# Cross-attention on one core: the context width as 128 + 64 rows instead of 96 + 96, with the 64-row products alternating between the two halves of TensorE's rows

## The chip, the cores and the metric

One NeuronCore of a Trainium2 chip runs the whole program. The metric is device time in microseconds (us) of one execution, as the median of several runs. TensorE (PE in the profile) does the matrix products, from SBUF into PSUM; VectorE (DVE) and ScalarE (ACT) empty PSUM and do the elementwise work; GpSimd (POOL) does one multiplication per tile; SyncE (SP) issues most transfers.

## What is computed

Everything is float32: 16 batches, 256 queries of width 256, 77 context rows of width 192, 8 heads of width 256.

```
Q = (img_embed @ Wq)   K = (sent_embed @ Wk)   V = (sent_embed @ Wv)     # 8 heads each
score = jnp.einsum('bhqd,bhkd->bhqk', Q, K) / math.sqrt(D)
score = jnp.where(mask, score, -jnp.inf)
attn = jax.nn.softmax(score, axis=-1)
ctx = jnp.einsum('bhqk,bhkd->bqhd', attn, V).reshape(B, -1, H * D)
out = ctx @ Wo + img_embed
mu = jnp.mean(out, axis=-1, keepdims=True)
var = jnp.var(out, axis=-1, keepdims=True)
return (out - mu) * jax.lax.rsqrt(var + EPS) * gamma + beta
```

## The kernel before

Neither Q, K, V nor the context of a head is formed. Per head h the kernel takes, once, `G_h = Wq_h Wk_h^T / sqrt(D)` and `U_h = Wv_h Wo_h`. Then, for a batch b, `A_bh = G_h c_b^T` (tile `a`) and `VW_bh = c_b U_h` (tile `vw`); the scores are `x_b A_bh` and the output is the sum over heads of `softmax(score) VW_bh`.

The products `a` and `vw` sum over the context width, 192. The kernel before takes it in two chunks of `LP` = 96 rows, so each of these products is two matmuls into one PSUM bank. A float32 matmul is two instructions on TensorE (each a weight load and a pass that streams the moving operand); a transpose is one. "Pass" below means one such instruction. So a product of `a` or `vw` is four passes.

The program has two parts.

- **Once** (lines 97 to 189): per head, transposes of Wq and Wk (`p_wqT`, `p_wkT`), their copies to SBUF, then `pg` (8 passes) and one copy of it into `gT`; six tiles of transposes of the context (`pc`), each with two copies into `cT`; per head, a transpose of Wv (`p_wvT`), `pu` (8 passes) and one copy into `u`.
- **The batches** (lines 192 to 336), in 32 steps t of 128 queries, two for each batch, eight for each group of four batches. At the first step of a group, `prepare_group` transposes x (`px`) and makes the 16 products `pa` of 308 columns, each copied by ACT or DVE in turn into `a`. Each step takes the scores (`ps`, 8 passes, two banks), then on DVE the bias is added (this reads `ps`), the maximum is taken and subtracted, ACT takes the exponential `e`, DVE the sum and reciprocal, POOL the product `p`. At each even step `prepare_batch` makes four products `pv` of 512 columns, each copied by ACT into `vw`. Two steps later `attend` transposes `p` (`pp`, two tiles of four), ACT copies them to `pT`, and `po` (16 passes) sums the heads; DVE adds x. `normalise_group` and the stores follow once a group.

Each engine runs its instructions in program order, which the scheduler of the language fixes when the kernel is built, by the order of the code, priorities and free buffers. PSUM has eight banks: `ps_sc` two buffers of two banks (scores), `ps_tr` two of one bank (all transposes), `ps_mm` two of one bank (`pg`, `pu`, `pa`, `pv`, `po`). A matmul into a buffer waits until the copy out of it is done.

Of the kernel before, what the change touches and what calls it, by code (L numbers as in the profile page):

```python
# [8 lines left out]
F32 = mybir.dt.float32  # L9
I32 = mybir.dt.int32  # L10
AF = mybir.ActivationFunctionType
ALU = mybir.AluOpType
AX = mybir.AxisListType
PSUM = bass.MemoryType.PSUM

P = 128
H = 8          # heads
D = 256        # head width
EPS = 1e-05
GB = 4         # batches in a group  # L20
MASKED = 3.0e38  # taken from a masked score: any score of less than 1e31 is absorbed by it


# Per head h the products are taken in this order:
#   G_h = Wq_h Wk_h^T / sqrt(D)        U_h = Wv_h Wo_h        (once)
#   A_bh = G_h c_b^T                   VW_bh = c_b U_h        (once a batch)
#   score_bh = x_b A_bh                out_b = sum_h softmax(score_bh) VW_bh
# so neither Q, K, V nor the context of a head is ever formed.
@with_exitstack
def kernel(  # L30
    ctx: ExitStack,
# [12 lines left out]
    nc = tc.nc  # L44
    B, S, DI = x.shape
    S2, DL = c.shape[1], c.shape[2]
    LP = DL // 2               # the context width goes in two chunks of LP rows
    CR = 112                   # rows of the flat context in one transpose
    NCR = B * S2 // CR
    NG = B // GB  # L50
    QT = S // P                # query tiles of a batch
    NT = B * QT
    GT = GB * QT               # query tiles of a group
    HK = H // 2 * S2           # score columns in one PSUM bank
    assert NCR * CR == B * S2 and NG * GB == B and DI == 2 * P and D == 2 * P

    const = ctx.enter_context(tc.tile_pool(name="const", bufs=1))
    xp = ctx.enter_context(tc.tile_pool(name="xp", bufs=2))
    ps_sc = ctx.enter_context(tc.tile_pool(name="ps_sc", bufs=2, space=PSUM))
    ps_tr = ctx.enter_context(tc.tile_pool(name="ps_tr", bufs=2, space=PSUM))  # L60
    ps_mm = ctx.enter_context(tc.tile_pool(name="ps_mm", bufs=2, space=PSUM))

    ident = const.tile([P, P], F32, tag="ident", name="ident")
    make_identity(nc, ident)
    eps = const.tile([P, 1], F32, tag="eps", name="eps")
    nc.vector.memset(eps, EPS)

    gT = const.tile([LP, 2, H, DI], F32, tag="gT", name="gT")
    u = const.tile([LP, 2, H, DI], F32, tag="u", name="u")
    cT = const.tile([LP, 2, B * S2], F32, tag="cT", name="cT")  # L70
    bias = const.tile([P, B, S2], F32, tag="bias", name="bias")
    live = const.tile([P, B], F32, tag="live", name="live")
    gam = const.tile([P, DI], F32, tag="gam", name="gam")
# [15 lines left out]
    def evacuate(dst, src):  # L89
        evacs[0] += 1  # L90
        if evacs[0] % 2:
            nc.scalar.copy(dst, src)  # L92
        else:
            nc.vector.tensor_copy(dst, src)  # L94

# [1 line left out]
    with tc.tile_pool(name="wload", bufs=1) as wp, tc.tile_pool(name="wt", bufs=2) as wt:  # L97
        wq_sb = wp.tile([P, 2, H * D], F32, tag="wq", name="wq_sb")
        wk_sb = wp.tile([LP, 2, H * D], F32, tag="wk", name="wk_sb")
        wv_sb = wp.tile([LP, 2, H * D], F32, tag="wv", name="wv_sb")  # L100
        wo_sb = wp.tile([P, 2 * H, DI], F32, tag="wo", name="wo_sb")
        c_sb = wp.tile([CR, NCR, DL], F32, tag="c", name="c_sb")
        m_i = wp.tile([P, B * S2], I32, tag="mi", name="m_i")
        wq_r = wq.rearrange("(t p) f -> p t f", p=P)
        wk_r = wk.rearrange("(t p) f -> p t f", p=LP)
        wv_r = wv.rearrange("(t p) f -> p t f", p=LP)
        half = H * D // 2
        for i in range(2):
            cols = slice(i * half, (i + 1) * half)
# [26 lines left out]
        for h in range(H):  # L136
            wqT = transposed(wq_sb, P, h, "wqT")
            wkT = transposed(wk_sb, LP, h, "wkT")
            pg = ps_mm.tile([P, 2, DI], F32, tag="mm", name=f"pg_{h}")
            for lc in range(2):  # L140
                for dc in range(2):
                    nc.tensor.matmul(  # L142
                        pg[:LP, lc, :],
                        wkT[:, dc, lc * LP : (lc + 1) * LP],
                        wqT[:, dc, :],
                        start=(dc == 0),
                        stop=(dc == 1),
                    )
            nc.scalar.mul(gT[:, :, h, :], pg[:LP], D ** -0.5)

        for r in range(0, NCR, 2):
            n = min(2, NCR - r)
            pc = ps_tr.tile([P, 4, P], F32, tag="tr", name=f"pc_{r}")
            for lc in range(2):
                for j in range(n):
                    nc.tensor.transpose(
                        pc[:LP, 2 * lc + j, :CR],
                        c_sb[:, r + j, lc * LP : (lc + 1) * LP],
                        ident[:CR, :CR],
                    )  # L160
            for lc in range(2):
                evacuate(
                    cT[:, lc, r * CR : (r + n) * CR].rearrange("p (j m) -> p j m", m=CR),
                    pc[:LP, 2 * lc : 2 * lc + n, :CR],
                )

        for h in range(H):
            wvT = transposed(wv_sb, LP, h, "wvT")
            pu = ps_mm.tile([P, 2, DI], F32, tag="mm", name=f"pu_{h}")
            for lc in range(2):  # L170
                for dc in range(2):
                    nc.tensor.matmul(  # L172
                        pu[:LP, lc, :],
                        wvT[:, dc, lc * LP : (lc + 1) * LP],
                        wo_sb[:, 2 * h + dc, :],
                        start=(dc == 0),
                        stop=(dc == 1),
                    )
            evacuate(u[:, :, h, :], pu[:LP])

        # bias: 0 where the mask is nonzero, -MASKED where it is zero, which exp takes to 0.
        # live: 1 for a batch with an unmasked column, else 0 / 0, the NaN of the reference.
        bias_f = bias.rearrange("p b k -> p (b k)")
        nc.vector.tensor_scalar(bias_f, m_i, 0.0, None, ALU.not_equal)
        some = wp.tile([P, B], F32, tag="some", name="some")
# [2 lines left out]
        nc.vector.tensor_tensor(live, live, some, ALU.mult)  # L188
        nc.vector.tensor_scalar(bias_f, bias_f, 1.0, MASKED, ALU.subtract, ALU.mult)

# [1 line left out]
    ap = ctx.enter_context(tc.tile_pool(name="ap", bufs=2))  # L192
    sp = ctx.enter_context(tc.tile_pool(name="sp", bufs=3))
    st = ctx.enter_context(tc.tile_pool(name="st", bufs=4))
# [3 lines left out]
    def prepare_group(g):  # L198
        xg = xg_of[g]
        xT = xp.tile([P, 2, GT * P], F32, tag="xT", name=f"xT_{g}")  # L200
        for j in range(0, GT, 2):
            pt = ps_tr.tile([P, 4, P], F32, tag="tr", name=f"px_{g}_{j}")
            for dc in range(2):
                for i in range(2):
                    nc.tensor.transpose(  # L205
                        pt[:, 2 * dc + i, :], xg[:, j + i, dc * P : (dc + 1) * P], ident
                    )
            evacuate(
                xT[:, :, j * P : (j + 2) * P],
                pt.rearrange("p (dc i) m -> p dc (i m)", dc=2),  # L210
            )
        xT_of[g] = xT
        a = ap.tile([P, 2, GB, H, S2], F32, tag="a", name=f"a_{g}")
        for h in range(H):
            for dc in range(2):
                pa = ps_mm.tile([P, GB, S2], F32, tag="mm", name=f"pa_{g}_{h}_{dc}")
                for lc in range(2):
                    nc.tensor.matmul(  # L218
                        pa.rearrange("p b k -> p (b k)"),
                        gT[:, lc, h, dc * P : (dc + 1) * P],  # L220
                        cT[:, lc, g * GB * S2 : (g + 1) * GB * S2],
                        start=(lc == 0),
                        stop=(lc == 1),
                    )
                evacuate(a[:, dc, :, h, :], pa)
        a_of[g] = a
        mv_of[g] = st.tile([P, GT, 2], F32, tag="mv", name=f"mv_{g}", bufs=2)

    def prepare_batch(b):
        vw = ap.tile([S2, H, DI], F32, tag="vw", name=f"vw_{b}", bufs=3)  # L230
        for n in range(H // 2):
            pv = ps_mm.tile([P, 2 * DI], F32, tag="mm", name=f"pv_{b}_{n}")
            for lc in range(2):
                nc.tensor.matmul(  # L234
                    pv[:S2],
                    cT[:, lc, b * S2 : (b + 1) * S2],
                    u[:, lc, 2 * n : 2 * n + 2, :].rearrange("p h d -> p (h d)"),
                    start=(lc == 0),
                    stop=(lc == 1),
                )  # L240
            nc.scalar.copy(vw[:, 2 * n : 2 * n + 2, :].rearrange("p h d -> p (h d)"), pv[:S2])  # L241
        vw_of[b] = vw

    def scores_and_softmax(t):
# [78 lines left out]
    for t in range(NT + AHEAD):  # L323
# [6 lines left out]
        if t >= AHEAD:  # L330
            d = t - AHEAD
# [36 lines left out]
```

## Time and profile before

| | |
|---|---|
| median of 3 runs | 482.4 us (482.24 to 482.61) |
| span of the profiled execution, first to last instruction | 480.1 us |
| median less span | 2.3 us |
| TensorE busy | 439.0 us, 91% of the span |
| VectorE, ScalarE, GpSimd busy | 210.7, 136.8 and 39.6 us |
[...]

The profiled execution has no time of its own in the results beside its span; 2.3 us is what lies around the span if it ran like the median. Busy time of TensorE includes the modelled end of each matmul, so it doesn't tell how much of that time is needed.

### The profile page before, as it was taken

The numbers are of one execution on the slowest core, as the hardware profiler recorded it, in microseconds if no ns is written. First come the engines' busy times: TensorE is split into PE (matmuls) and PEld (weight loads), VectorE is DVE, ScalarE is ACT, GpSimd is POOL, SyncE is SP. The second block draws the span as 40 slices with busy tenths as digits, with TensorE's granted clock in tenths as the row PEclk, the third lists the DMA queues.
The fourth block names the chain that finished last, engine by engine and source line by source line (L and its number), as shares of the span: only waits on it lengthen the run. The fifth ranks groups of instructions, "written<-read, shape, count | busy, mean of one in ns | idle before, by whom it ended". The sixth has DMA issues, their size and how long they took to land.

```text
span 480.1 us, 4689 instructions
## 1 busy us (share of the span) xinstructions
PE 439.0 (91%) x1846; PEld 298.3 (62%) x1846; DVE 210.7 (44%) x424; ACT 136.8 (28%) x242; POOL 39.6 (8%) x38
## 2 busy tenths in 40 slices
PE   1409899999999999999999999999999999999993
PEld 1307677755765875758567766585767756658572
DVE  0031223235736433375373433844735238555364
ACT  1103422223132222251333213523132134331321
POOL 0000000012112000121111101112111011121110
PEclk9859999999999999999999999999999999999997
DMA  8993000000000000022000000130000000200002
GB/s 237 256 341 106 0 1 1 0 2 0 0 1 0 1 0 0 1 87 89 0 0 1 0 0 2 53 123 0 1 1 0 1 0 1 89 0 0 2 1 87
DMA packets 13446, 17.86 MB, mean 37 GB/s; under 512 B 480, under 2 KB 12208, under 8 KB 13232
## 3 DMA queue, kind: packets, MB, share of 16 engines
q1 hardware_dynamic: 9696, 12.95, 8.9%
q10 hardware_dynamic: 3728, 4.62, 3.3%
q8 instruction: 14, 0.23, 0.2%
q14 instruction: 8, 0.07, 0.0%
HBM read 13.37 MB, written 4.19 MB: 37 GB/s over the span
## 4 chain that ended last, share of the span: by engine, by line
PE 87%; DMA 6%; DVE 3%; ACT 2%; issue 0%; DVEq 0%; ACTq 0%
PE po L293 24%; PE pv L234 22%; PE pa L218 14%; PE ps L250 14%; PE pp L289 5%; DMA m_i<-in_mask_BxS_if_dram 5%; PE pg L142 3%; PE pu L172 3%; DMA wk_sb<-in_L_xattn_Wk_dram 2%; PE px L205 2%; DVE wkT L94 1%; ACT pT L290 1%; DVE xg L313 1%; PE p_wkT L126 0%; PE p_wvT L126 0%
## 5 line engine op out<-in xcount | busy, mean ns | idle before, releaser
L293 PE MATMUL po<-vw,pT 77*128 77x256 f32 x512 | 117.2, 382 | 1.7 <-ACT pT L290 1.7
L234 PE MATMUL pv<-u,cT 96*77 96x512 f32 x256 | 113.1, 593 | 0.1
L293 PEld LDWEIGHTS po<-vw,pT 77*128 77x128 f32 x512 | 94.6, 190 | 21.3 <-ACT pT L290 9.7
L234 PEld LDWEIGHTS pv<-u,cT 96*77 96x77 f32 x256 | 37.5, 148 | 67.0 <-issue 57.8
L250 PE MATMUL ps<-a,xT 128*128 128x308 f32 x256 | 75.8, 422 | 0.0
L277 POOL TENSOR_TENSOR p<-e,rden 128x616 f32<-128x616 f32 x32 | 38.9, 1216 | 423.1 <-DVE rden L275 236.5
L218 PE MATMUL pa<-cT,gT 96*128 96x308 f32 x256 | 67.7, 422 | 0.0
L241 ACT COPY vw<-pv 77x512 f32<-77x512 f32 x64 | 37.1, 581 | 97.8 <-PE pv L234 97.5
L297 DVE TENSOR_TENSOR xg<-po,xg 128x256 f32<-128x256 f32 x32 | 13.6, 424 | 108.8 <-PE po L293 108.7
L290 ACT COPY pT<-pp 77x512 f32<-77x512 f32 x64 | 34.1, 583 | 86.5 <-PE pp L289 86.5
L218 PEld LDWEIGHTS pa<-cT,gT 96*128 96x128 f32 x256 | 48.0, 190 | 16.6
L250 PEld LDWEIGHTS ps<-a,xT 128*128 128x128 f32 x256 | 46.5, 190 | 12.4 <-issue 0.5
L289 PEld LDWEIGHTS pp<-ident,p 128*77 128x77 f32 x256 | 30.4, 148 | 11.3 <-issue 5.3
L94 DVE COPY a<-pa 128x308 f32<-128x308 f32 x32 | 15.3, 479 | 48.1 <-PE pa L218 48.1
L272 DVE TENSOR_REDUCE den<-e 128x8 f32<-128x616 f32 x32 | 25.4, 794 | 23.5 <-ACT e L270 23.4
L142 PE MATMUL pg<-wqT,wkT 128*96 128x256 f32 x64 | 18.9, 447 | 18.2 <-DVE wkT L94 18.2
L289 PE MATMUL pp<-ident,p 128*77 128x128 f32 x256 | 33.2, 272 | 0.0
L258 DVE TENSOR_TENSOR s<-ps,bias 128x616 f32<-128x616 f32 x32 | 25.6, 799 | 10.7 <-PE ps L250 10.7
L270 ACT ACTIVATE e<-s 128x616 f32<-128x616 f32 x32 | 22.9, 717 | 23.5 <-DVE s L266 23.4
L92 ACT COPY a<-pa 128x308 f32<-128x308 f32 x32 | 13.4, 418 | 48.3 <-PE pa L218 48.3
L142 PEld LDWEIGHTS pg<-wqT,wkT 128*96 128x96 f32 x64 | 11.6, 192 | 23.5 <-DVE wkT L94 19.8
L266 DVE TENSOR_TENSOR s<-s,top 128x616 f32<-128x616 f32 x32 | 25.6, 800 | 1.0
(45 smaller groups left out, 212.8 us busy)
## 6 DMA issues: line engine op xcount, KB each, us to landing
xg<-in_x_dram SPq DMA_DIRECT2D x4, 1024.0 KB, 12.5
out_dram<-xg SPq DMA_DIRECT2D x16, 256.0 KB, 2.2
wq_sb<-in_L_xattn_Wq_dram SPq DMA_DIRECT2D x2, 1024.0 KB, 12.3
wo_sb<-in_L_xattn_Wo_dram ACTq DMA_DIRECT2D x1, 2048.0 KB, 39.0
wk_sb<-in_L_xattn_Wk_dram ACTq DMA_DIRECT2D x2, 768.0 KB, 11.3
wv_sb<-in_L_xattn_Wv_dram SPq DMA_DIRECT2D x1, 1536.0 KB, 22.1
c_sb<-in_ctx_dram ACTq DMA_DIRECT2D x1, 924.0 KB, 27.3
m_i<-in_mask_BxS_if_dram SPq DMA_DIRECT2D x1, 616.0 KB, 21.7
```

The costliest lines, as they stand in the source:

```text
L142: nc.tensor.matmul(pg[:LP, lc, :], wkT[:, dc, lc * LP : (lc + 1) * LP], wqT[:, dc, :], start=(dc == 0), stop=(dc == 1),)
L218: nc.tensor.matmul(pa.rearrange("p b k -> p (b k)"), gT[:, lc, h, dc * P : (dc + 1) * P], cT[:, lc, g * GB * S2 : (g + 1) * GB * S2], star ...
L234: nc.tensor.matmul(pv[:S2], cT[:, lc, b * S2 : (b + 1) * S2], u[:, lc, 2 * n : 2 * n + 2, :].rearrange("p h d -> p (h d)"), start=(lc == 0 ...
L241: nc.scalar.copy(vw[:, 2 * n : 2 * n + 2, :].rearrange("p h d -> p (h d)"), pv[:S2])
L250: nc.tensor.matmul(ps[:, hh, :HK], xT_of[g][:, dc, j * P : (j + 1) * P], a_of[g][:, dc, bl, hh * 4 : hh * 4 + 4, :].rearrange("p h k -> p ...
L258: nc.vector.tensor_tensor(s.rearrange("p (a h) k -> p a h k", a=2), ps[:, :, :HK].rearrange("p a (h k) -> p a h k", k=S2), bias[:, b, :].u ...
L266: nc.vector.tensor_tensor(s, s, top.unsqueeze(2).to_broadcast([P, H, S2]), ALU.subtract)
L272: nc.vector.tensor_reduce(den, e, AX.X, ALU.add)
L277: nc.gpsimd.tensor_tensor(p, e, rden.unsqueeze(2).to_broadcast([P, H, S2]), ALU.mult)
L289: nc.tensor.transpose(pt[:S2, i, :], p[:, hh * 4 + i, :], ident)
L290: nc.scalar.copy(pT[:, hh * 4 : hh * 4 + 4, :], pt[:S2])
L293: nc.tensor.matmul(po, pT[:, h, :], vw_of[b][:, h, :], start=(h == 0), stop=(h == H - 1))
```

## The change

The context width goes in one chunk of 128 rows (`gA`, `uA`, `cA`) and one of 64 (`gB`, `uB`, `cB`). A product of `a` or `vw` is a matmul over 128 rows and one over 64 rows. The 64-row operands stand in rows 0 to 63 or in rows 64 to 127: `gB` by the head's parity, `uB` by the parity of the pair of heads, and `cB` in both halves. Products are made four at a time, in four banks: first the four 128-row matmuls, then the four 64-row ones, whose halves alternate from one matmul to the next, then the four copies. `ps_mm` gets four buffers, and `ps_sc` one instead of two. In the first part each PSUM tile of `pg`, `pu` and `pc` is emptied by two or three copies instead of one or two. `ps`, `pp`, `po` and the softmax are as before.

```
-    ps_sc = ctx.enter_context(tc.tile_pool(name="ps_sc", bufs=2, space=PSUM))
+    ps_sc = ctx.enter_context(tc.tile_pool(name="ps_sc", bufs=1, space=PSUM))
-    ps_mm = ctx.enter_context(tc.tile_pool(name="ps_mm", bufs=2, space=PSUM))
+    ps_mm = ctx.enter_context(tc.tile_pool(name="ps_mm", bufs=4, space=PSUM))
...
-                        pg[:LP, lc, :],
-                        wkT[:, dc, lc * LP : (lc + 1) * LP],
+                        pg[:, lc, :],
+                        wkT[:, dc, lc * LB : lc * LB + P],
...
-            nc.scalar.mul(gT[:, :, h, :], pg[:LP], D ** -0.5)
+            nc.scalar.mul(gA[:, h, :], pg[:, 0, :], D ** -0.5)
+            half = slice(h % 2 * LB, h % 2 * LB + LB)
+            nc.vector.tensor_scalar(gB[half, h // 2, :], pg[LB:, 1, :], D ** -0.5, None, ALU.mult)
...
+            evacuate(cA[:, rows].rearrange("p (j m) -> p j m", m=CR), pc[:, :n, :CR])
+            for i in range(2):
                 evacuate(
-                    cT[:, lc, r * CR : (r + n) * CR].rearrange("p (j m) -> p j m", m=CR),
-                    pc[:LP, 2 * lc : 2 * lc + n, :CR],
+                    cB[i * LB : (i + 1) * LB, rows].rearrange("p (j m) -> p j m", m=CR),
+                    pc[LB:, 2 : 2 + n, :CR],
                 )
...
-            evacuate(u[:, :, h, :], pu[:LP])
+            evacuate(uA[:, h, :], pu[:, 0, :])
+            n = h // 2
+            evacuate(uB[n % 2 * LB : n % 2 * LB + LB, n // 2, h % 2, :], pu[LB:, 1, :])
...
+        for n in range(H // 2):
+            parts = [(dc, i) for dc in range(2) for i in range(2)]
+            pa = {
+                (dc, i): ps_mm.tile([P, GB, S2], F32, tag="mm", name=f"pa_{g}_{2 * n + i}_{dc}")
+                for dc, i in parts
+            }
+            for dc, i in parts:
+                nc.tensor.matmul(
+                    pa[dc, i].rearrange("p b k -> p (b k)"),
+                    gA[:, 2 * n + i, dc * P : (dc + 1) * P],
+                    cA[:, cols],
+                    start=True,
+                    stop=False,
+                )
+            for dc, i in parts:
+                half = slice(i * LB, (i + 1) * LB)
+                nc.tensor.matmul(
+                    pa[dc, i].rearrange("p b k -> p (b k)"),
+                    gB[half, n, dc * P : (dc + 1) * P],
+                    cB[half, cols],
+                    start=False,
+                    stop=True,
+                )
+            for dc, i in parts:
+                evacuate(a[:, dc, :, 2 * n + i, :], pa[dc, i])
...
+        pv = [ps_mm.tile([P, 2 * DI], F32, tag="mm", name=f"pv_{b}_{n}") for n in range(H // 2)]
         for n in range(H // 2):
...
+            nc.tensor.matmul(
+                pv[n][:S2],
+                cA[:, cols],
+                uA[:, 2 * n : 2 * n + 2, :].rearrange("p h d -> p (h d)"),
+                start=True,
+                stop=False,
+            )
+        for n in range(H // 2):
+            half = slice(n % 2 * LB, n % 2 * LB + LB)
+            nc.tensor.matmul(
+                pv[n][:S2],
+                cB[half, cols],
+                uB[half, n // 2, :, :].rearrange("p h d -> p (h d)"),
+                start=False,
+                stop=True,
+            )
+        for n in range(H // 2):
+            nc.scalar.copy(
+                vw[:, 2 * n : 2 * n + 2, :].rearrange("p h d -> p (h d)"), pv[n][:S2]
+            )
```

Three places show how the scheduler then orders the work. Rows name the line, the operation, output and inputs (with a tile's running number) and what the instruction waits for; a matmul row is two passes, a transpose row (`pp`, `p_wkT`) one, and "x3" means three such.

TensorE in the third batch (steps 4 and 5), from the products `vw` to the start of `po`, before:

```order
L234 MATMUL pv_0_704<-u,cT 77x512 [waits DVE_49]
L234 MATMUL pv_0_704<-u,cT 77x512
L234 MATMUL pv_1_708<-u,cT 77x512 [waits DVE_49]
L234 MATMUL pv_1_708<-u,cT 77x512
L234 MATMUL pv_2_712<-u,cT 77x512 [waits Activation_49]
L234 MATMUL pv_2_712<-u,cT 77x512
L234 MATMUL pv_3_716<-u,cT 77x512 [waits Activation_49]
L234 MATMUL pv_3_716<-u,cT 77x512
```

The same place after the change, with the step's transposes `pp`, the first matmul of the next scores and the first of `po`:

```order
L261 MATMUL pv_2_731<-uA,cA 77x512
L261 MATMUL pv_3_732<-uA,cA 77x512 [waits DVE_49]
L270 MATMUL pv_0_729<-uB,cB 77x512
L270 MATMUL pv_1_730<-uB,cB 77x512
L270 MATMUL pv_2_731<-uB,cB 77x512
L270 MATMUL pv_3_732<-uB,cB 77x512
L328 MATMUL pp_0_746<-ident,p_619 77x128 [waits PE_49,Pool_49]
L328 MATMUL pp_0_746<-ident,p_619 77x128 x3
L328 MATMUL pp_1_752<-ident,p_619 77x128 [waits PE_49]
L328 MATMUL pp_1_752<-ident,p_619 77x128 x3
L289 MATMUL ps_771<-a_481,xT_456 128x308 [waits DVE_49]
L332 MATMUL po_758<-vw_621,pT_745 128x256 [waits Activation_49]
```

All four products now end among the last four matmuls of `pv`, where before one ended after each two matmuls; what follows them is unchanged.

ScalarE in the same batch, from the exponential to the copies `pT`, before:

```order
L241 COPY vw_703<-pv_0_704 77x512 [waits PE_49]
L270 ACTIVATE e_694<-s_689 128x616 [waits DVE_49,Pool_49]
L241 COPY vw_703<-pv_1_708 77x512 [waits PE_49]
L241 COPY vw_703<-pv_2_712 77x512 [waits PE_49]
L241 COPY vw_703<-pv_3_716 77x512 [waits PE_49]
L290 COPY pT_720<-pp_0_721 77x512 [waits PE_49,Activation_49]
L290 COPY pT_720<-pp_1_727 77x512 [waits PE_49]
```

And after:

```order
L309 ACTIVATE e_719<-s_714 128x616 [waits DVE_49,Pool_49]
L278 COPY vw_728<-pv_0_729 77x512 [waits PE_49]
L278 COPY vw_728<-pv_1_730 77x512 [waits PE_49]
L278 COPY vw_728<-pv_2_731 77x512 [waits PE_49]
L278 COPY vw_728<-pv_3_732 77x512 [waits PE_49]
L329 COPY pT_745<-pp_0_746 77x512 [waits PE_49,Activation_49]
L329 COPY pT_745<-pp_1_752 77x512 [waits PE_49]
```

The exponential moved ahead of the four copies `vw`; the copies `pT` still stand behind all four.

VectorE in the first part, heads 3 to 6 (`wkT` is the copy that `pg` of the head waits for), before:

```order
L94 COPY wkT_177<-p_wkT_178 128x384 [waits DVE_49,PE_49]
L94 COPY wkT_197<-p_wkT_198 128x384 [waits DVE_49,PE_49]
L94 COPY wkT_217<-p_wkT_218 128x384 [waits DVE_49,PE_49]
L94 COPY wkT_237<-p_wkT_238 128x384 [waits DVE_49,PE_49]
L94 COPY wkT_257<-p_wkT_258 128x384 [waits DVE_49,PE_49]
```

And after:

```order
L101 COPY wkT_183<-p_wkT_184 128x384 [waits DVE_49,PE_49]
L158 TENSOR_SCALAR gB<-pg_190 64x256 [waits Activation_49]
L101 COPY wkT_204<-p_wkT_205 128x384 [waits DVE_49,PE_49]
L158 TENSOR_SCALAR gB<-pg_211 64x256 [waits Activation_49]
L101 COPY wkT_225<-p_wkT_226 128x384 [waits DVE_49,PE_49]
L158 TENSOR_SCALAR gB<-pg_232 64x256 [waits Activation_49]
L101 COPY wkT_246<-p_wkT_247 128x384 [waits DVE_49,PE_49]
```

Each copy `wkT` now stands behind the second copy of the head before, which itself waits for ScalarE's copy out of the same `pg`.

## Rows read from the trace of the kernel before

**Rows 1.** The page's first part: span; busy time, share of span, instructions.

```profile
span 480.1 us, 4689 instructions
PE 439.0 (91%) x1846; PEld 298.3 (62%) x1846; DVE 210.7 (44%) x424; ACT 136.8 (28%) x242; POOL 39.6 (8%) x38
```

**Rows 2.** The page's chain that ended last: shares by engine, then by line.

```profile
PE 87%; DMA 6%; DVE 3%; ACT 2%; issue 0%; DVEq 0%; ACTq 0%
PE po L293 24%; PE pv L234 22%; PE pa L218 14%; PE ps L250 14%; PE pp L289 5%; DMA m_i<-in_mask_BxS_if_dram 5%; PE pg L142 3%; PE pu L172 3%; DMA wk_sb<-in_L_xattn_Wk_dram 2%; PE px L205 2%; DVE wkT L94 1%; ACT pT L290 1%; DVE xg L313 1%; PE p_wkT L126 0%; PE p_wvT L126 0%
```

**Rows 3.** Costliest groups: shapes xcount | busy us, mean ns | idle before.

```profile
L234 PE MATMUL pv<-u,cT 96*77 96x512 f32 x256 | 113.1, 593 | 0.1
...
L250 PE MATMUL ps<-a,xT 128*128 128x308 f32 x256 | 75.8, 422 | 0.0
...
L218 PE MATMUL pa<-cT,gT 96*128 96x308 f32 x256 | 67.7, 422 | 0.0
L241 ACT COPY vw<-pv 77x512 f32<-77x512 f32 x64 | 37.1, 581 | 97.8 <-PE pv L234 97.5
```

**Rows 4.** Chain in order of time: start us, us, what (passes).

```profile
80.55 16.07 PE pa L218 x62
96.62 2.07 PE ps L250 x8
...
149.17 6.87 PE pv L234 x16
156.04 0.88 PE pp L289 x8
...
157.44 3.49 PE po L293 x16
...
163.65 3.72 PE po L293 x16
```

**Rows 5.** Timeline of that batch: start, us, engine, line, operation [idle before].

```profile
156.08 0.58 ACT L241 COPY vw<-pv 77x512 f32<-77x512 f32 x1 [1.13 <-PE pv L234]
...
156.57 1.06 ACT L290 COPY pT<-pp 77x512 f32<-77x512 f32 x2
...
157.20 3.32 PEld L293 LDWEIGHTS po<-vw,pT 77*128 77x128 f32 x16 [0.26 <-ACT pT L290]
...
163.01 1.06 ACT L290 COPY pT<-pp 77x512 f32<-77x512 f32 x2 [5.38 <-PE pp L289]
...
163.64 3.32 PEld L293 LDWEIGHTS po<-vw,pT 77*128 77x128 f32 x16 [0.52 <-ACT pT L290]
```

**Rows 6.** Timeline after an odd step: transposes, bias add, next scores' weights.

```profile
122.85 1.04 PE L289 MATMUL pp<-ident,p 128*77 128x128 f32 x8
123.05 0.80 DVE L258 TENSOR_TENSOR s<-ps,bias 128x616 f32<-128x616 f32 x1
...
123.62 0.30 PEld L250 LDWEIGHTS ps<-a,xT 128*128 128x128 f32 x2
```

**Rows 7.** Timeline of the first part.

```profile
44.35 0.50 PE L126 MATMUL p_wkT<-ident,wk_sb 96*128 96x96 f32 x4
44.55 0.59 ACT L149 ACTIVATE gT<-pg 96x512 f32<-96x512 f32 x1 [1.54 <-PE pg L142]
...
44.88 0.56 DVE L94 COPY wkT<-p_wkT 128x384 f32<-128x384 f32 x1 [2.39 <-PE p_wkT L126]
...
57.65 0.97 PE L156 MATMUL pc<-ident,c_sb 112*96 112x112 f32 x8 [0.57 <-DVE cT L94]
...
60.59 3.69 PE L172 MATMUL pu<-wo_sb,wvT 128*96 128x256 f32 x16
```

**Rows 8.** Groups by line of ACT and DVE in the first part.

```profile
L92 ACT COPY wvT<-p_wvT 128x384 f32<-128x384 f32 x8 | 3.5, 482 | 11.6 <-PE p_wvT L126 11.6
...
L94 DVE COPY u<-pu 96x512 f32<-96x512 f32 x8 | 5.5, 686 | 13.4 <-PE pu L172 13.4
...
L94 DVE COPY wkT<-p_wkT 128x384 f32<-128x384 f32 x8 | 4.5, 556 | 26.9 <-PE p_wkT L126 26.9
```

More of the change, by code (lines that the diff above doesn't have):

```diff
@@ L47 @@
     LP = DL // 2
+    LA = P
+    LB = DL - LA
     CR = 112
@@ L54 @@
     HK = H // 2 * S2
-    assert NCR * CR == B * S2 and NG * GB == B and DI == 2 * P and D == 2 * P
+    assert NCR * CR == B * S2 and NG * GB == B and DI == 2 * P and D == 2 * P and 2 * LB == P
     const = ctx.enter_context(tc.tile_pool(name="const", bufs=1))
     xp = ctx.enter_context(tc.tile_pool(name="xp", bufs=2))
-    ps_sc = ctx.enter_context(tc.tile_pool(name="ps_sc", bufs=2, space=PSUM))
+    ps_sc = ctx.enter_context(tc.tile_pool(name="ps_sc", bufs=1, space=PSUM))
     ps_tr = ctx.enter_context(tc.tile_pool(name="ps_tr", bufs=2, space=PSUM))
-    ps_mm = ctx.enter_context(tc.tile_pool(name="ps_mm", bufs=2, space=PSUM))
+    ps_mm = ctx.enter_context(tc.tile_pool(name="ps_mm", bufs=4, space=PSUM))
     ident = const.tile([P, P], F32, tag="ident", name="ident")
@@ L66 @@
     nc.vector.memset(eps, EPS)
-    gT = const.tile([LP, 2, H, DI], F32, tag="gT", name="gT")
-    u = const.tile([LP, 2, H, DI], F32, tag="u", name="u")
-    cT = const.tile([LP, 2, B * S2], F32, tag="cT", name="cT")
+    gA = const.tile([LA, H, DI], F32, tag="gA", name="gA")
+    gB = const.tile([P, H // 2, DI], F32, tag="gB", name="gB")
+    uA = const.tile([LA, H, DI], F32, tag="uA", name="uA")
+    uB = const.tile([P, H // 4, 2, DI], F32, tag="uB", name="uB")
+    cA = const.tile([LA, B * S2], F32, tag="cA", name="cA")
+    cB = const.tile([P, B * S2], F32, tag="cB", name="cB")
     bias = const.tile([P, B, S2], F32, tag="bias", name="bias")
@@ L156 @@
                     nc.tensor.transpose(
-                        pc[:LP, 2 * lc + j, :CR],
-                        c_sb[:, r + j, lc * LP : (lc + 1) * LP],
+                        pc[:, 2 * lc + j, :CR],
+                        c_sb[:, r + j, lc * LB : lc * LB + P],
                         ident[:CR, :CR],
                     )
-            for lc in range(2):
+            rows = slice(r * CR, (r + n) * CR)
+            evacuate(cA[:, rows].rearrange("p (j m) -> p j m", m=CR), pc[:, :n, :CR])
+            for i in range(2):
                 evacuate(
-                    cT[:, lc, r * CR : (r + n) * CR].rearrange("p (j m) -> p j m", m=CR),
-                    pc[:LP, 2 * lc : 2 * lc + n, :CR],
+                    cB[i * LB : (i + 1) * LB, rows].rearrange("p (j m) -> p j m", m=CR),
+                    pc[LB:, 2 : 2 + n, :CR],
                 )
@@ L172 @@
                     nc.tensor.matmul(
-                        pu[:LP, lc, :],
-                        wvT[:, dc, lc * LP : (lc + 1) * LP],
+                        pu[:, lc, :],
+                        wvT[:, dc, lc * LB : lc * LB + P],
                         wo_sb[:, 2 * h + dc, :],
@@ L213, in prepare_group @@
         a = ap.tile([P, 2, GB, H, S2], F32, tag="a", name=f"a_{g}")
[L214 to L225, printed above, removed]
+        cols = slice(g * GB * S2, (g + 1) * GB * S2)
+        for n in range(H // 2):
[23 more added lines that the diff above has]
+                evacuate(a[:, dc, :, 2 * n + i, :], pa[dc, i])
         a_of[g] = a
@@ L230, in prepare_batch @@
         vw = ap.tile([S2, H, DI], F32, tag="vw", name=f"vw_{b}", bufs=3)
+        cols = slice(b * S2, (b + 1) * S2)
+        pv = [ps_mm.tile([P, 2 * DI], F32, tag="mm", name=f"pv_{b}_{n}") for n in range(H // 2)]
         for n in range(H // 2):
[L232 to L241, printed above, removed]
+            nc.tensor.matmul(
[18 more added lines that the diff above has]
+            )
         vw_of[b] = vw
```

## The prediction

> **What bounds the kernel now.** I read the page's first part, then the chain that ended last, then its pieces in order of time. The span is 480.1 us and TensorE is busy for 91% of it [rows 1]; in the chain it has 87%, and the four products of the batches (`po`, `pv`, `pa`, `ps`) alone have 74% [rows 2]. The other engines stand in the chain with a few per cent. So what counts is TensorE's time per pass, plus each moment in which it is made to wait.
>
> The chain's pieces give the time per pass: `pa` 16.07 / 62 = 0.2592 us, `pv` 6.87 / 16 = 0.4294 us [rows 4]. `pa` with 96 rows and `ps` with 128 rows and the same 308 columns take the same: 422 ns each as modelled, 2.07 / 8 = 0.259 us in the chain [rows 3, 4]. A pass costs columns, not rows. So 128 + 64 rows in place of 96 + 96 saves nothing by itself: as many passes, as long. The whole gain has to come from 64-row passes that run side by side on the two halves.
>
> **The change, part by part.**
>
> *The overlap.* A set of four products was 16 passes and still is: 8 over 128 rows, 8 over 64. The order of the 64-row passes is low, low, high, high, low, low, high, high, since each matmul is two passes on one half. If matmuls start in program order and two run together only on different halves, the slots are: low alone; low with high; high with low; low with high; high alone. That is 5 slots for 8 passes, 3 hidden. No row shows two matmuls at once, so this is bounded: 0 hidden if the halves exclude each other, 4 if every pair runs together. I take 3, which the order of the passes gives once the halves are independent. There are 16 sets of `pa` (4 groups, 4 pairs of heads) and 16 of `pv`: 16 x 3 x 0.2592 = 12.4 us and 16 x 3 x 0.4294 = 20.6 us.
>
> *The switches.* Each set changes from whole array to halves and back, 64 changes in all. What one costs no row shows. Below: nothing, if weights for the new shape are loaded ahead as now. The nearest row is `po` after a wait: 16 passes take 3.72 us where they take 3.49 us in an unbroken stream [rows 4], so a stream that must load its first weights in the open loses 0.23 us. Above: the last pass must also have landed first; a modelled pass of `pv` lasts 593 ns against 429 ns from start to start [rows 3, 4], a tail of 0.16, so 0.40. I take 0.23, since a restart is what a change of shape resembles most. For `pa` the gain falls to 16 x (0.778 - 0.46) = 5.1 us.
>
> [...]
>
> *`pv` and ScalarE.* Before, a `vw` copy starts 0.04 us after its product's end in the chain (156.04 to 156.08) and takes 0.58, and three of the four hide under `pv` [rows 4, 5]. Now the products end 1.29, 0.86 and 0.43 us before the end E of `pv`, and at E. Four copies of 0.58 in a row start at E - 1.25 and end at E + 1.08. Behind them on ScalarE stands `pT` (0.53), for which `po` waits: done at E + 1.61, and by the later row (163.01 + 0.53, weights at 163.64) the weights follow 0.10 later, at E + 1.71. Before, `po` began at E + 1.40 (157.44). So it comes 0.31 late, and with the restart of 0.23 that is 0.54 us [rows 4, 5]. The switch back to the whole array hides in this wait. 15 batches have a `pp` behind their `pv`. Net: 20.6 - 16 x 0.23 - 15 x 0.54 - 0.23 = 8.6 us. If all four pairs overlapped, the copies would end 0.4 us later still and eat the extra.
>
> *One score buffer.* After an odd step, `pp` takes 0.88 us (the piece before `po`) and the next scores begin at 122.85 + 0.88 = 123.73. DVE's bias add reads the last scores from 123.05 to 123.85 [rows 4, 6]. With two buffers that is hidden. With one, the weights load at about 123.93, 0.20 late, and in the open, 0.23: 0.43 us. It occurs 11 times (twice in the first group, three times in each later one; at group starts `pa` stands between, after even steps `pv`). 4.7 us. Bounds: 0.2 x 11 = 2.2 and 0.5 x 11 = 5.5.
>
> *The first part.* TensorE's passes are as many and as long. But the copy `wkT` now follows `gB`, which waits for `gA`. From the end of `pg` at 44.35, ScalarE's copy starts 0.20 later [rows 7]. Copies of 256 columns, scaled from 384 and 512, are 0.38 us on ScalarE and 0.42 on DVE [rows 3, 8]. `gA` ends at +0.58, `gB` at +1.05, and `wkT` starts at +1.05 where it now starts at +0.53 (44.88): 0.52 us for each of heads 4 to 7, 2.1 us. Heads 1 to 3 hide it, as two `pg` now stand in a row. The six `pc` tiles are emptied by three copies in turn on one tile instead of two; TensorE already waits there, 0.57 us at 57.65 [rows 7]. One more copy and hand-over, about 0.5, in three rounds: 1.5 us. For `pu`, which before ran two heads in a row (16 passes) [rows 7], copies now stand ahead of `wvT` on DVE; I count two more waits of 0.5. Together 4.5 us; between 0, if the order's cover is better than I see, and 9 if each wait is twice that.
>
> *At nothing:* the other copies of `pa` (the first bank is free about 0.52 + 0.20 + 0.42 = 1.14 us after the 64-row passes begin, its copy scaled as above; the next set wants it after 5 slots, 1.30, and a switch); the wider weights, which load under the pass before; the same transfers.
>
> **The sum.** 480.1 - 5.1 - 8.6 + 4.7 + 4.5 = 475.6 us of span, and with the 2.3 us by which the median stands above it, 477.9 us: 0.9% less.
>
> **The rivals.**
>
> *Dear switches.* The overlap works but each switch costs 0.40. Then `pa` loses 0.4 us in all, `pv` gains 20.6 - 6.4 - 8.1 - 0.4 = 5.7, and 9.2 are lost elsewhere: 484.0 of span, 486.3 us. The same comes out if the load for the other half can't start until the pass ahead of it has started. For it: a load starts about when the pass before starts, in all rows I saw. [...]
>
> *No overlap*, the other sign: the change doesn't do what it says. Passes on different halves run one after the other, `vw` copies keep pace as now, and all that stays is 64 switches and 9.2 us: 491.6 us with free switches, 506.3 with 0.23. It decides when fewer than about 2.6 of each set's 8 passes are hidden, for each hidden one is worth 16 x (0.2592 + 0.4294) = 11.0 us, against 9.2 + 14.7 + ScalarE's 4.7 beyond the switch. For it: the trace has never two matmuls in less than one pass's time. Against: it has never two on different rows, either.
>
> *Cheap switches.* With the weights loaded ahead and no drain, `pa` gains 12.4 and `pv` 12.5: 466.7 us. For it: in the stream from `pa` to `ps` or from `pv` to `pp` now, other tiles and shapes follow each other without loss (`pa` ends and `ps` begins at 96.62, `pv` ends and `pp` begins at 156.04) [rows 4]. Against: those are all whole-array passes.
>
> **How the numbers follow.** Forecast, with switches up to 0.23 and the cheap rival as its lower end (465 to 481): 0.50. Dear switches (481 to 490): 0.20. No overlap (490 to 508): 0.30. The likeliest is the first, and I give its time with the switch of the nearest row, 478 us; its own range is 465 to 481. The range leaves out the dearest third of "no overlap" and a twentieth below: 465 to 503. About 0.2% is what three runs of this kernel can tell from no change (they lie within 0.08%). Faster: nearly all of the first case and a little of the second, 0.52; within 0.2%: 0.05; slower, the third and most of the second: 0.43.
>
> **What would show it.** Overlap: the 64-row matmuls of a `pv` set begin in pairs, and eight of them take 2.1 to 2.2 us, not 3.4; for `pa` 1.3, not 2.1. Switch: the gap between the last whole pass and the first half pass beyond a pass's time. ScalarE: `po` after `pv` waiting for `pT`, 0.3 us idle. One score buffer: `ps` waiting for DVE's `s` after odd steps. First part: `pa` of the first group begins some 4.5 us later than at 80.55. I am wrong if the eight passes take as long as eight, or if a switch costs far from 0.23.

## The result, and the profile after

The changed kernel takes 466.76 us (465.88 to 467.32, 4 runs) against 482.32 us (482.10 to 482.61, 4 runs): ratio 0.9662, 95% interval 0.9638 to 0.9685. Faster, as forecast, and inside the range, but 3.4% where I had said 0.9%. The span fell from 480.1 to 464.8 us, by 15.3; I had 4.5.

The page of the changed kernel, its first part and the shares of its chain (by engine, by line), to be held against [rows 1, 2]:

```profile
span 464.8 us, 4714 instructions
PE 415.3 (89%) x1846; PEld 279.1 (60%) x1846; DVE 215.1 (46%) x439; ACT 132.7 (29%) x249; POOL 40.0 (9%) x38
...
PE 83%; DMA 7%; DVE 5%; ACT 4%; issue 1%; DVEq 0%; ACTq 0%
PE po L332 25%; PE ps L289 13%; PE pv L261 11%; PE pa L235 8%; PE pv L270 6%; PE pp L328 6%; DMA m_i<-in_mask_BxS_if_dram 5%; PE pa L244 4%; PE pu L183 4%; PE pg L149 3%; ACT pT L329 3%; DMA wk_sb<-in_L_xattn_Wk_dram 2%; PE px L218 2%; DVE xg L352 1%; DVE wkT L101 1%
```

TensorE runs as many instructions as before (1846), and `pa` has 12% of the chain where it had 14%, `pv` 17% where it had 22%. ScalarE rose from 2% to 4% and DVE from 3% to 5%: new waits. DVE's are in part those of the first group, where the chain now runs over the first steps' softmax (111.74 to 118.93 us) and before ran over `pv`.

Its chain in order of time, as in [rows 4]; L235 and L261 are the 128-row passes of `pa` and `pv`, L244 and L270 the 64-row ones:

```profile
91.19 2.33 PE pa L235 x8
93.51 1.24 PE pa L244 x8
94.75 2.32 PE pa L235 x8
...
126.66 0.87 PE pp L328 x8
127.53 0.02 issue
127.55 0.79 PE ps L289 x2
128.34 3.45 PE po L332 x16
...
133.35 3.43 PE pv L261 x8
136.78 1.88 PE pv L270 x8
138.66 1.04 PE pp L328 x8
...
139.74 0.61 ACT pT L329
...
140.40 3.72 PE po L332 x16
```

Eight 64-row passes of `pv` take 1.88 us and of `pa` 1.24 us. A slot is the time of one pass, 0.4294 and 0.2592 us. For `pv` that is four slots (1.72) and a little, not five (2.15) and not eight. For `pa` 1.24 by itself lies nearer to five slots (1.30) than to four (1.04), since a change of shape is in it; there the starts decide, in pairs at 89.88, 90.24, 90.50 and 90.76 us in its first set. The timeline of the `pv` batch shows the weights being loaded two at a time (PEld is a weight load):

```profile
136.71 0.21 PEld L270 LDWEIGHTS pv<-uB,cB 64*77 64x77 f32 x4 [0.80 <-issue]
136.72 1.95 PE L270 MATMUL pv<-uB,cB 64*77 64x512 f32 x8
137.21 0.15 PEld L270 LDWEIGHTS pv<-uB,cB 64*77 64x77 f32 x2 [0.28 <-issue]
...
137.83 2.03 ACT L278 COPY vw<-pv 77x512 f32<-77x512 f32 x4 [1.17 <-PE pv L270]
...
138.59 0.87 PEld L328 LDWEIGHTS pp<-ident,p 128*77 128x77 f32 x8 [0.80 <-issue]
```

Two loads in 0.15 us, the next two a pass later. In the whole trace all 128 such passes of `pv` and all 128 of `pa` start in pairs, at most 0.01 us apart. Ahead of the first load of the new shape, and of the first after it (138.59), the load queue stood still for 0.80 us; inside a shape it is 0.28. In all 32 sets the first pass of a new shape starts within 0.01 us of its load's start, on the way to the halves and on the way back: in this trace no weights are loaded ahead across a change of shape.

Step by step, the 15.3 us are these. `pa`: a set takes 2.33 + 1.24, from one set's start to the next 3.56 us, where 16 passes took 4.147: 16 x 0.587 = 9.4 us less. `pv`: 3.43 + 1.88 = 5.31 for 6.87, but `po` then starts 1.74 us after the end of `pv` (140.40) instead of 1.40, and takes 3.72 instead of 3.49: 15 x 0.99 + 1.56 = 16.4 less. Scores after an odd step: from the end of `ps` at 126.66 to `po` 1.68 us instead of 1.39 (123.02 to 124.41 in the chain before): 11 x 0.29 = 3.2 more. The first part: the sets of `pa` end at 101.87 where they ended at 96.62, and are themselves 4 x 0.587 shorter: 7.6 more. Sum: 15.0 less. It is made of typical pieces; 0.3 of the 15.3 us is left over.

### The profile page after: what moved, and what is told of

Its sections match the earlier page's. It is cut to its first block, busy times and chain, and to the rows that moved or that the text cites. A ratio compares the mean times of both kernels' runs of the same rounds, so it can differ in the third digit from the quotient of the medians.

```text
span 464.8 us, 4714 instructions
## 1 busy us (share of the span) xinstructions
PE 415.3 (89%) x1846; PEld 279.1 (60%) x1846; DVE 215.1 (46%) x439; ACT 132.7 (29%) x249; POOL 40.0 (9%) x38
## 4 chain that ended last, share of the span: by engine, by line
PE 83%; DMA 7%; DVE 5%; ACT 4%; issue 1%; DVEq 0%; ACTq 0%
PE po L332 25%; PE ps L289 13%; PE pv L261 11%; PE pa L235 8%; PE pv L270 6%; PE pp L328 6%; DMA m_i<-in_mask_BxS_if_dram 5%; PE pa L244 4%; PE pu L183 4%; PE pg L149 3%; ACT pT L329 3%; DMA wk_sb<-in_L_xattn_Wk_dram 2%; PE px L218 2%; DVE xg L352 1%; DVE wkT L101 1%
## 5 line engine op out<-in xcount | busy, mean ns | idle before, releaser
L289 PE MATMUL ps<-a,xT 128*128 128x308 f32 x256 | 77.6, 429 | 0.2
L261 PE MATMUL pv<-uA,cA 128*77 128x512 f32 x128 | 57.7, 592 | 0.0
L328 PEld LDWEIGHTS pp<-ident,p 128*77 128x77 f32 x256 | 29.2, 147 | 14.9 <-issue 12.0
L235 PE MATMUL pa<-cA,gA 128*128 128x308 f32 x128 | 37.7, 432 | 0.0
L149 PE MATMUL pg<-wqT,wkT 128*128 128x256 f32 x64 | 19.0, 454 | 19.9 <-DVE wkT L101 19.9
L261 PEld LDWEIGHTS pv<-uA,cA 128*77 128x77 f32 x128 | 18.9, 148 | 29.5 <-issue 22.2
L278 ACT COPY vw<-pv 77x512 f32<-77x512 f32 x64 | 32.4, 586 | 14.0 <-PE pv L270 14.0
L101 DVE COPY a<-pa 128x308 f32<-128x308 f32 x32 | 15.3, 479 | 37.4 <-PE pa L244 36.7
L270 PE MATMUL pv<-uB,cB 64*77 64x512 f32 x128 | 31.1, 605 | 0.0
L235 PEld LDWEIGHTS pa<-cA,gA 128*128 128x128 f32 x128 | 22.7, 190 | 11.7 <-ACT a L99 5.7
L149 PEld LDWEIGHTS pg<-wqT,wkT 128*128 128x128 f32 x64 | 14.2, 232 | 23.4 <-DVE wkT L101 21.1
```

Source lines behind the costliest of these rows:

```text
L149: nc.tensor.matmul(pg[:, lc, :], wkT[:, dc, lc * LB : lc * LB + P], wqT[:, dc, :], start=(dc == 0), stop=(dc == 1),)
L235: nc.tensor.matmul(pa[dc, i].rearrange("p b k -> p (b k)"), gA[:, 2 * n + i, dc * P : (dc + 1) * P], cA[:, cols], start=True, stop=False,)
L261: nc.tensor.matmul(pv[n][:S2], cA[:, cols], uA[:, 2 * n : 2 * n + 2, :].rearrange("p h d -> p (h d)"), start=True, stop=False,)
L270: nc.tensor.matmul(pv[n][:S2], cB[half, cols], uB[half, n // 2, :, :].rearrange("p h d -> p (h d)"), start=False, stop=True,)
L289: nc.tensor.matmul(ps[:, hh, :HK], xT_of[g][:, dc, j * P : (j + 1) * P], a_of[g][:, dc, bl, hh * 4 : hh * 4 + 4, :].rearrange("p h k -> p ...
L328: nc.tensor.transpose(pt[:S2, i, :], p[:, hh * 4 + i, :], ident)
```

## The experiments

My first theory (T): the two halves are independent streams; each runs its own passes, whatever the other half has ahead of it in the program; the rest of the time is the changes of shape, ScalarE's queue, one score buffer and the first part. Its rivals stand with each run.

**All 64-row operands on one half.** `gB` and `uB` get one half-height tile each, all matmuls of 64 rows use rows 0 to 63.

```
-                half = slice(i * LB, (i + 1) * LB)
+                half = slice(0, LB)
...
-            half = slice(n % 2 * LB, n % 2 * LB + LB)
+            half = slice(0, LB)
```

> All 64-row operands stand in rows 0 to 63, so no two 64-row passes can be on different halves; banks, order, copies and the 64 changes between whole array and half stay. If the gain comes from passes that run side by side: eight 64-row passes take eight slots again (pv 3.4 us, pa 2.1 us), and what is left is the cost of the changes, read as about 0.16 us each in the changed kernel, one score buffer and the first part: some 502 us. If a change costs 0.23 as I predicted, 506 us. Rival: a 64-row pass is simply twice as fast by itself: then the time stays at 467 us.

Measured: 502.17 us, ratio 1.0420 (1.0397 to 1.0443). Its chain:

```profile
91.43 2.27 PE pa L234 x8
93.70 2.27 PE pa L243 x8
...
107.31 3.43 PE pv L260 x8
110.75 3.59 PE pv L269 x8
```

Eight 64-row passes take as long as eight 128-row ones. So the passes aren't faster; it is the second half that gives the time. Between this run and the changed kernel lie 35 us, the whole gain and more. A set of `pv` is 7.02 us where it was 6.87, one of `pa` 4.54 where it was 4.147: without overlap, the 128 + 64 split only costs.

**Low, low, high, high.**

```
-            for dc, i in parts:
+            for i, dc in [(i, dc) for i in range(2) for dc in range(2)]:
...
-        for n in range(H // 2):
+        for n in (0, 2, 1, 3):
             half = slice(n % 2 * LB, n % 2 * LB + LB)
```

> The same four 64-row matmuls of each set, ordered low, low, high, high: four passes on the low half stand ahead of the first on the high half. If each half runs its own passes without regard to what the other half has ahead of it: 4 slots for 8 passes as in the changed kernel, 467 us. If a pass can get past only the two passes of one matmul: 5 slots, one more in each of 32 sets, 11 us more, 478 us. If passes start strictly in program order (my prediction's assumption): 7 slots, 33 us more less the waits for ScalarE that this removes, 490 to 500 us.

Measured: 471.23 us, ratio 0.9770 (0.9753 to 0.9788): between T and the rivals. The chain tells why:

```profile
136.28 1.93 PE pv L270 x8
138.21 0.60 ACT vw L278 x2
138.81 0.34 issue
...
140.27 0.92 PE po L332 x3
```

The eight passes still take four slots, though all four passes of one half now stand ahead of the other half's first. The weight loads of that batch come in twos as before:

```profile
136.21 0.22 PEld L270 LDWEIGHTS pv<-uB,cB 64*77 64x77 f32 x4 [0.80 <-issue]
136.71 0.16 PEld L270 LDWEIGHTS pv<-uB,cB 64*77 64x77 f32 x2 [0.27 <-issue]
```

In the whole trace all 64-row passes start in pairs again, 0.013 to 0.015 us apart. Two passes on one half don't run together (the run before), so one of each pair is on the other half. So TensorE takes the first pass of the free half ahead of three that still wait before it in the program; the fourth starts with it.

What came late is ScalarE: `po` starts 2.06 us after the end of `pv`, not 1.74; 15 x 0.32 = 4.8 us. The first copy starts as before, the second waits. The reason is in the signals (semaphore updates) that the copies wait for: in this run TensorE gives them in program order, though its passes don't run in it. In this batch the trace has one signal at 137.31 us and three at 138.17 to 138.25; the changed kernel has two at 137.81 and 137.85 and two at 138.67 and 138.71. The first product on the free half is done in the second slot, but stands third in the program and is reported behind the one ahead of it. The copies of `pa` show the same. There ScalarE copies the products made on the low half, DVE those made on the high half, since both alternate from product to product. The changed kernel first, then this run:

```profile
90.70 0.94 ACT L99 COPY a<-pa 128x308 f32<-128x308 f32 x2 [2.64 <-PE pa L244]
90.74 1.00 DVE L101 COPY a<-pa 128x308 f32<-128x308 f32 x2 [1.10 <-PE pa L244]
```

```profile
90.19 0.94 ACT L99 COPY a<-pa 128x308 f32<-128x308 f32 x2 [2.64 <-PE pa L244]
...
90.75 0.87 DVE L101 COPY a<-pa 128x308 f32<-128x308 f32 x2 [1.62 <-PE pa L244]
```

DVE starts 0.04 us after ScalarE there and 0.56 us after it here. Whether ScalarE's wait is all that this order costs, the run with this order and two engines tests below.

**The kernel before with one score buffer.**

```
-    ps_sc = ctx.enter_context(tc.tile_pool(name="ps_sc", bufs=2, space=PSUM))
+    ps_sc = ctx.enter_context(tc.tile_pool(name="ps_sc", bufs=1, space=PSUM))
```

> The kernel before with one score buffer instead of two, nothing else. By the changed kernel's chain the next scores after an odd step start 0.29 us later, 11 times: 3.2 us, 485.5 us. By the prediction's 0.43 us: 487 us. Rival: the wait is hidden (po waits for pT anyway): 482.3 us.

Measured: 484.93 us, ratio 1.0054 (1.0039 to 1.0070), 2.9 us more. Its chain has the two lines that the changed kernel has: `issue` 0.02 and two passes of `ps` in 0.79 instead of 0.52.

```profile
124.41 0.02 issue
124.43 0.79 PE ps L250 x2
```

The wait itself is nearly nothing; that the weights load in the open, 0.27 us, is the price.

**The first part's copies dealt out anew.**

```
-            nc.vector.tensor_scalar(gB[half, h // 2, :], pg[LB:, 1, :], D ** -0.5, None, ALU.mult)
+            nc.scalar.mul(gB[half, h // 2, :], pg[LB:, 1, :], D ** -0.5)
...
+            nc.scalar.copy(cA[:, rows].rearrange("p (j m) -> p j m", m=CR), pc[:, :n, :CR])
+            nc.vector.tensor_copy(
+                cB[LB:, rows].rearrange("p (j m) -> p j m", m=CR), pc[LB:, 2 : 2 + n, :CR]
+            )
+            nc.gpsimd.tensor_copy(cB[:LB, rows], cB[LB:, rows])
...
-            evacuate(uA[:, h, :], pu[:, 0, :])
+            nc.vector.tensor_copy(uA[:, h, :], pu[:, 0, :])
...
-            evacuate(uB[n % 2 * LB : n % 2 * LB + LB, n // 2, h % 2, :], pu[LB:, 1, :])
+            nc.vector.tensor_copy(uB[n % 2 * LB : n % 2 * LB + LB, n // 2, h % 2, :], pu[LB:, 1, :])
```

The copies `wqT` and `wvT` go to ScalarE, `wkT` to DVE.

> The changed kernel with the copies of its first part dealt out so that no copy for TensorE stands behind a second copy of another tile on the same engine: gA and gB both on ScalarE, wkT on DVE, wvT on ScalarE, uA and uB on DVE; cA on ScalarE, the upper half of cB on DVE, its lower half copied from SBUF by GpSimd. If the first part's 7.6 us of loss is those waits and the lower clock that follows them, nearly all comes back: 460 us. Rival: the loss is in the third copy and in wider tiles as such, only the wkT part (2 to 3 us) comes back: 464 us.

Measured: 460.62 us, ratio 0.9551 (0.9532 to 0.9571): 6 of the 7.6 us come back. Part of that is clock. In the changed kernel (window from the start of `pu`: its bounds and length, busy us of each engine, granted clock, transfers):

```profile
65.50:87.60 22.10, 21.24 (x105) 17.73 (x105) 5.50 (x13) 5.11 (x13) 0.00 (x0) 0.88 0.00 1
```

In the kernel before, the same stretch, that of `pu`:

```profile
60.60:80.00 19.40, 18.52 (x104) 14.23 (x104) 6.18 (x9) 3.65 (x8) 0.00 (x0) 1.00 0.00 1
```

And in this experiment, where the stretch begins within the last `pc`:

```profile
60.00:80.00 20.00, 18.73 (x105) 15.89 (x106) 7.26 (x19) 3.96 (x11) 1.02 (x3) 1.00 0.00 1
```

In the changed kernel TensorE waits for the third copies out of `pc`, 1.39 and 1.24 us; from 61.40 to 63.70 us it is busy for 1.06 of 2.30. After that it runs part of `pu` at a granted clock of 0.50; in the later piece, from 84.57 us, it is 1.00. From its timeline (one of the waits), its windows and its chain:

```profile
61.39 0.99 PE L165 MATMUL pc<-ident,c_sb 112*128 112x112 f32 x8 [1.39 <-ACT cB L99]
```

```profile
65.25:68.74 3.49, 3.49 (x9) 2.67 (x9) 0.00 (x0) 0.00 (x0) 0.00 (x0) 0.50 0.00 0
```

```profile
65.46 3.49 PE pu L183 x8
...
84.57 1.99 PE pu L183 x8
```

Eight passes of `pu` take 3.49 us there and 1.99 us later. The seven other runs with the changed kernel's first part have a granted clock of 0.66 or 0.83 from 62 to 72 us, the changed kernel 0.66; the kernel before and the two runs with the copies dealt out anew have 1.00. How much of the 6 us is the clock and how much the waits themselves, no run separates.

**The copies `vw` on two engines.**

```
-            nc.scalar.copy(
+            evacuate(
                 vw[:, 2 * n : 2 * n + 2, :].rearrange("p h d -> p (h d)"), pv[n][:S2]
             )
```

> The changed kernel with the four copies vw of a batch dealt out to ScalarE and DVE in turn, nothing else. If po comes late after each pv because pT stands behind four copies on ScalarE (0.57 us, 15 times), pT starts about 0.45 us sooner and most of it comes back: 459 to 460 us. Rival: DVE, which has the softmax to do, delays its two copies or the softmax as much: 466 to 468 us.

Measured: 459.42 us, ratio 0.9522 (0.9508 to 0.9536). In its chain `po` follows without ScalarE, and takes 3.49 again:

```profile
137.91 1.03 PE pp L328 x8
138.93 0.52 PE ps L289 x2
139.45 3.49 PE po L332 x16
```

**Sets of two in two banks.** Both pools back to two buffers, products two at a time.

```
-        for n in range(H // 2):
-            parts = [(dc, i) for dc in range(2) for i in range(2)]
+        for n, c2 in [(n, c2) for n in range(H // 2) for c2 in range(2)]:
+            parts = [(c2, i) for i in range(2)]
...
+        for m in range(0, H // 2, 2):
+            pv = {
+                n: ps_mm.tile([P, 2 * DI], F32, tag="mm", name=f"pv_{b}_{n}") for n in (m, m + 1)
+            }
```

> Sets of two products (one on each half) in two banks instead of four in four; two score buffers again. 64 more changes between whole array and half at 0.16 us, 10 us; the next set's first matmul waits for a copy out of one of the two banks: some 0.45 us in each of 32 more sets of pa, 15 us, and 0.6 in each pv, 10 us; 3 us back from the scores: some 499 us. Rival: copies hide as they did before the change, and what matters is only that the halves run side by side: 474 us.

Measured: 513.61 us, ratio 1.0641 (1.0625 to 1.0656), worse than both. For `pa` it did not test what it should: with two banks, and as I read it because each product gets its bank as one comes free, the scheduler takes apart 28 of the 32 pairs. Its chain of `pa`:

```profile
94.01 0.71 PE pa L235 x2
94.73 0.71 PE pa L244 x2
```

Two passes over 128 rows, two over 64, and so on: nothing to run side by side, and a change of shape after every second pass. Of the pairs of `pv` 31 of 32 stay together, but there TensorE waits for copies out of the two banks (us in total, times, longest):

```profile
PE pv L264 <- ACT vw L281: 9.9, 16, 0.7
```

Against the run with sets of two in four banks below, where two products of `pa` take 1.95 us instead of 2.86, that is 28 x 0.91 = 25 us and 9.9 us of the 39 between them. So the four banks keep the pairs of `pa` together in the order, and keep TensorE from waiting in `pv`.

**A change with each product.** Each 64-row matmul directly behind its 128-row one, four banks.

```
-            for dc, i in parts:
                 half = slice(i * LB, (i + 1) * LB)
...
-        for n in range(H // 2):
             half = slice(n % 2 * LB, n % 2 * LB + LB)
```

> Each 64-row matmul directly behind its own 128-row matmul: 8 changes of shape in a set instead of 2, and no two 64-row matmuls next to each other. Against the kernel with all 64-row operands on one half (502.2 us), which has no overlap either, there are 6 more changes in each of 32 sets. At 0.16 us each, as the changed kernel's chain shows: 31 us more, 533 us. At 0.23, as I predicted: 546 us. If a change costs nothing and the 0.16 are the start of two passes at once: 502 us.

Measured: 536.14 us, ratio 1.1115 (1.1097 to 1.1134). Against the run with one half, 34.0 us for 6 x 32 = 192 changes: 0.177 us each. Its chain gives it by shape:

```profile
93.67 0.71 PE pa L243 x2
94.38 0.71 PE pa L235 x2
...
127.57 1.01 PE pv L268 x2
128.58 1.01 PE pv L260 x2
```

`pa`: 1.42 for four passes of 0.2592, 0.19 a change. `pv`: 2.02 for four of 0.4294, 0.15. In the changed kernel's profile a weight load of 128 columns lasts 190 ns (L235), one of 77 columns 148 (L261): the change costs about the load, which isn't hidden there. That is an agreement of numbers; no run separates it from the end of the last pass (the prediction's tail of 0.16 us).

**Sets of two in four banks**, one score buffer; otherwise as above with two.

> Sets of two products, one on each half, with four banks and one score buffer as in the changed kernel (so the scheduler can keep pairs together, which it did not with two banks). 2 more changes of shape for each of the 32 sets of four, 64 in all. At 0.16 to 0.18 us: 10 to 11 us more; half of the copies vw now hide under the second pair, so pT waits some 0.2 us less in 15 batches, 3 us: some 474 us. Rival: the halves need four or more passes each in the queue to run side by side, and the overlap is lost or halved: 490 us or more.

Measured: 474.70 us, ratio 0.9848 (0.9829 to 0.9868). The pairs stay together and run side by side, four passes in two slots (0.86 us for `pv`, 0.52 for `pa`) and a change, and twice the changes cost what they should (the two of a set of `pa` 1.23 + 0.72 - 6 x 0.2592 = 0.39 us, the one into the halves in `pv` 1.02 - 0.86 = 0.16):

```profile
89.63 1.23 PE pa L235 x4
90.86 0.72 PE pa L244 x4
...
134.76 1.72 PE pv L264 x4
136.47 1.02 PE pv L273 x4
```

**Low, low, high, high, with `vw` on two engines.** The edits of the second and fifth run together.

> The order low, low, high, high and the copies vw on two engines. With that order the changed kernel took 4.5 us longer though eight 64-row passes took as long. If all of it is ScalarE's second copy, which waits until the third product is done as well and so delays pT and po: with two engines little of it is left, 459 to 461 us (459.4 with the alternating order). Rival: the order costs TensorE something in each set: 464 us.

Measured: 459.35 us, ratio 0.9531 (0.9516 to 0.9545), as with the alternating order (459.42). So the 4.5 us were ScalarE's; the order costs TensorE nothing that these runs can tell.

**The first part and `vw` together.** The edits of the fourth and fifth run.

> The changed kernel with the copies of the first part dealt out anew (460.6 us by itself) and the copies vw on two engines. If the two losses are separate, the gains add: 453 us. Rival: vw on two engines gains nothing or what it gains is lost to DVE: 460 us or more.

Measured: 453.81 us, ratio 0.9405 (0.9386 to 0.9424). The two losses are separate and their gains add. This version beats both kernels.

## Why the prediction was off, step by step

- **The overlap** is the step that failed. "If matmuls start in program order and two run together only on different halves" gave 3 hidden passes of 8, and I said: "I take 3". All 4 are hidden. The second clause held (one half: no overlap), the first didn't: the order low, low, high, high still takes four slots. The part ahead of the prediction says the same, that each engine runs its instructions in program order; for TensorE's passes on different halves it is wrong. One more hidden pass in each set is 16 x 0.2592 = 4.1 us for `pa` and 16 x 0.4294 = 6.9 us for `pv`, 11.0 us, where the span differs from the forecast by 10.8; the other misses nearly cancel. That the 6.9 us of `pv` reached the span at all hangs on ScalarE, third point. I had the bound of 4 and dropped it on an assumption about issue order that no row bore out; the trace of before had only matmuls over the same rows, which by the run with one half follow each other in any case (eight passes in 3.59 us). The second run contradicts the assumption, for passes on different halves (eight in 1.93 us); the signals of their ends do come in program order there (one at 137.31 us, three from 138.17).
- **The switches**: predicted 0.23 us, measured 0.15 to 0.19 by shape and 0.177 on average. For `pa` two changes and a short wait for a copy out of a bank come to 3.56 - 12 x 0.2592 = 0.45, where I had 0.46. The trace shows that the stream stops at a change (ahead of the first load the load queue stands still for 0.80 us in `pv`, 0.28 inside a shape), and the price is below my middle value.
- **ScalarE and `po`**: predicted 0.54 us a batch, measured 0.57, so near by luck. By the run with two engines, which gives back 7.3 of the 15 x 0.57 = 8.6 us, it is this queue. Two errors met in it: the products end earlier, in pairs, and the four copies follow each other every 0.48 us (2.03 us in all), not every 0.58, since a copy begins about 0.1 us before the one ahead has ended. The prediction held that with all four pairs side by side the copies would "eat the extra" of `pv`; this is the second step that failed. Four copies of 0.58 from 0.83 us before the end of `pv` would have let `po` start 2.12 us after it (an estimate: 4 x 0.58 - 0.83, and the prediction's 0.53 and 0.10); it started after 1.74. So the shorter spacing kept 15 x 0.38 = 5.7 of the 6.9 us.
- **One score buffer**: predicted 0.43 us, 4.7 in all; measured 0.29 and 3.2 (2.9 in the kernel before). The weights in the open I had right (0.27 for 0.23); the 0.20 of lateness was wrong, because I held DVE's end against the start of a pass, 0.16 us before the chain's own count.
- **The first part**: predicted 4.5 us, measured 7.6, the term that was too small. That the copies cause it is shown, since dealing them out anew gives 6 back. From the end of the last `pg` (56.15 before, 59.07 after) 2.9 us against 2.1: the period of a head is 3.52 us (2.95 before, and 0.52 worked out), but head 3 already came 0.9 late. `pc` 1.7 against 1.5. `pu` 2.9 against 1.0: here the clock was not in my sum. Two pieces of `pu` that later take 1.99 and 3.72 us took 3.49 and 4.10, 1.9 of the 2.9.
- **The rivals**: "No overlap" was priced at 491.6 to 506.3 us; the run on one half is that case, 502.2. "Dear switches" is refuted by the 0.177. "Cheap switches" gave 466.7 us, the time measured, by chance: it had 3 hidden passes and changes at no cost; measured are 4 and 0.177 us.

## What to carry to other kernels

Float32 products over 64 rows on the two halves run side by side in this kernel, in pairs, in both orders of a set that were run (eight passes of `pv` in 1.88 to 1.93 us), as long as both halves' passes stand next to each other with nothing of the whole array between (directly behind its 128-row passes each two of `pv` took 1.01 us, a change of shape included). Make sets as large as banks allow, since each change of shape cost 0.15 to 0.19 us here, about one weight load. Look at the order that is built: with two banks the scheduler took the pairs of `pa` apart, and the kernel was slower than before. Then look at who empties the banks: products that end together put their copies in a row on one engine, and what stands behind them there becomes the next wait (four copies `vw` in 2.03 us, and `po` 0.34 us later). In the order low, low, high, high a product that ran ahead on the free half was reported only behind the one ahead of it in the program, and with all copies `vw` on ScalarE that order took 4.5 us more: alternate the halves.

## What was not expected of the hardware

- TensorE takes a pass on the free half ahead of passes that stand before it in the program, three of them waiting in the order low, low, high, high, float32 passes with their weight loads: eight passes of 0.4294 us in 1.88 to 1.93 us in either order. Its signals still come in program order (one at 137.31 us, three from 138.17).
- Waits of 1.39 and 1.24 us in a stretch of short transposes are followed by a granted clock of 0.88 in the next stretch, 0.50 at its start; eight passes of `pu` took 3.49 us instead of 1.99. With the first part dealt out anew the clock was 1.00.
- A copy of 512 columns on ScalarE lasts 0.58 us, but four in a row take 2.03 us: 0.48 each and one tail.
